# A graph attention layer on one core: the third weight slice as seven 128-cubed products per block product, PSUM in pairs of banks, ten weight sums kept resident

## The chip, the cores and the metric

The kernel runs on one core of a Trainium2 chip, in float32 throughout. The metric is the device time of one execution in microseconds; a lower time is better. The engines are named as in the profile: PE (matrix products; PEld is its weight load), DVE (vector), ACT (activation), POOL (GpSimd), SP (issues most of the DMAs).

## The reference

```python
# x: (128, 128, 768), adj: (128, 128, 128), Wq/Wk/Wv: (768, 768); H = 12 heads of 64
h = maximum(layernorm(x), 0)
q, k, v = (split_heads(h @ W + b) for W, b in ((Wq, bq), (Wk, bk), (Wv, bv)))
scores = einsum('bhqd,bhkd->bhqk', q, k) / 8 + beta * adj[:, None]
scores = where(adj[:, None] > 0, scores, -9e15)
out = einsum('bhqk,bhkd->bhqd', softmax(scores, -1), v)
return x + merge_heads(out)
```

## The kernel before

The 128 batch elements are worked on in 32 groups of four (`GRP = 4`, `NG = 32`). The weights' 2304 output columns are three slices of 768: `qk0` (first half of Q and K), `v`, and `qk1` (second half of Q and K). For a group and a slice, the activations form a 2 x 3 grid of blocks A00 to A12 (each 256 by 256: two batch elements by two chunks of 128 input features), the weights a 3 x 3 grid B00 to B22. A fast algorithm multiplies the grids with 15 block products instead of 18: `PRODUCTS` lists for each the activation operand (a block A.. or a sum S.. of blocks, `SUMS_A`), the weight operand (a block B.. or a sum T.., `SUMS_B`), the accumulation chain in PSUM (a, b, c or d) and the output tiles (r, j) that the chain's state is added to or subtracted from.

In the slices `qk0` and `v` each block product is split once more, into seven products of 128-cubed blocks ("zones") in place of eight (`product_z`, matmuls at line 495). That needs four further inner sums of the activation operand, which POOL makes (`inner`, lines 418 to 421), and seven prepared parts of the weight operand, which are made once (`prepare`), stored in DRAM, and streamed in again for every group through a ring of five tiles (`load_T`, line 297; `RING = 5`). The chain's state takes two PSUM banks (zones 0 to 3 and 4 to 6). An output tile is opened by copies from PSUM (lines 508 to 517) and then added to (DVE, lines 521 and 522). When its last product is in, POOL decodes the zones into Q and K or V (`decode`, lines 540 to 556); that is put off to the following product's slot by `later`.

In the slice `qk1` each block product is four matmuls of 256 columns per half of the output rows with resident weights (`product`, matmuls at line 571): its state takes one PSUM bank, tiles are opened by two ACT copies (line 581) and added to by one DVE instruction (line 587), and nothing has to be decoded. PE's array is used in two halves of 64 columns in all of these.

The order of the work is written out by hand. A slice is run as 15 slots, one block product each (`run`): the product's matmuls, then the steps that `then` put at that slot, then what is due (`weighing`, `overdue`), then the additions from PSUM, then the slot's "post" steps. Within an engine instructions are issued in this order. Scores of a half of the heads (`scores`, lines 609 to 616) follow early in the next slice; attention of a pair of heads (`attend`, line 646) is started at the slots `AV_AT` in `qk1` and `AV_Z` in `qk0`, and its matmuls are put singly between those of the products (`turn`). `weigh` (lines 623 to 630) divides by the softmax sums: three small DVE instructions and four ACT copies per half tile. For the next group the same slots hold the normalisation of x (`norm`, ACT), its transposition (`to_hT`, DVE line 406), the sums (`sum_acts`, DVE line 411) and the statistics of the group after (`row_stats`).

```python
AV_AT = (5, 8, 11)
AV_Z = (7, 9, 12)
ZORDER = (0, 4, 2, 8, 1, 6, 5, 3, 10, 7, 13, 9, 11, 12, 14)
free = deque(psum.tile([P, W], F32, name=f"bank{i}") for i in range(8))
take, give = free.popleft, free.append
```

The first group runs all three slices without the fast algorithm (`plain_slice`), while the weight sums are prepared. The last group's `qk1` slice has its attention and its last half-tile stores worked in.

Of the kernel before, what the change touches and what calls it, by code (L numbers as in the profile page):

```python
# [96 lines left out]
HOME = {"B00": "T12", "B10": "T10", "B02": "T0", "B20": "T4", "B11": "T13"}  # L97

SC_AT = 1
AV_AT = (5, 8, 11)
AV_Z = (7, 9, 12)
# [3 lines left out]
ZORDER = (0, 4, 2, 8, 1, 6, 5, 3, 10, 7, 13, 9, 11, 12, 14)  # L107
RING = 5

LAST = (0, 1, 2, 3, 5, 7, 6, 10, 11, 9, 4, 12, 8, 13, 14)  # L110
# [4 lines left out]
def direct(ctx, tc, x, adj, wq, bq, wk, bk, wv, bv, beta, out, bad):  # L115
# [34 lines left out]
    xg, xp, A, SP, biasT, vt, qk = {}, {}, {}, {}, {}, {}, {}  # L150

    def home_x(G, g):
        if not g % 2:
            xp[G, g // 2] = work.tile([P, 2 * NB, QD], F32, tag="x", name=f"x_{G}_{g}", bufs=2)
        t = xg[G, g] = xp[G, g // 2][:, (g % 2) * NB:(g % 2 + 1) * NB, :]
        return t

    def load_x(G, r):
        for g in range(2):
            home_x(G, 2 * r + g)  # L160
        src = x[G * GRP + 2 * r:G * GRP + 2 * r + 2].rearrange("g (b i) (a f) -> a i (g b) f", i=SQ, a=NB)
        for a in range(NB):
            nc.sync.dma_start(xp[G, r][a * SQ:(a + 1) * SQ], src[a])


    for g in range(2):
        t = home_x(0, g)
# [3 lines left out]
    ident = const.tile([P, P], F32, name="ident")  # L171
    make_identity(nc, ident)
    mean8 = const.tile([P, NB, SQ], F32, name="mean8")
# [6 lines left out]
    seen = const.tile([P, 20], F32, name="seen")  # L180

    over = const.tile([P, 44], F32, name="over")
# [7 lines left out]
    spbuf = const.tile([P, len(PRODUCTS), GRP, P], F32, name="spbuf")  # L190
# [8 lines left out]
    def flat(lo, hi):  # L199
        return spbuf[:, lo:hi].rearrange("p s g n -> p (s g n)")  # L200

    def raw_qk(u, t, parts):

        v = t.rearrange("p (c i j n) -> p c i j n", c=NC, i=2, j=3)
        for lo, hi in parts:
            for i, name in enumerate(("q", "k")):
                load_cols(nc.sync, v[:, :, i, lo:hi].rearrange("p c j n -> p c (j n)"), name, (lo + 3 * u) * P)
# [4 lines left out]
    def raw_v():  # L212
        t = flat(9, 15).rearrange("p (c n) -> p c n", c=NC)
        load_cols(nc.sync, t, "v", 0)
        for k in range(3):
            own = work.tile([P, GRP, P], F32, tag="xo", name=f"v_B{k}2", bufs=3)
            own = own.rearrange("p (c i) n -> p c (i n)", c=2)
            load_cols(nc.sync, own, "v", 4 * P, slice(2 * k, 2 * k + 2))
            for j in range(3):
                b = t[:, 2 * k:2 * k + 2, j * 2 * P:(j + 1) * 2 * P] if j < 2 else own  # L220
                wt["v", f"B{k}{j}"] = b.rearrange("p c (i n) -> p c i n", i=2)
# [7 lines left out]
    def sum_weights(sl, n):  # L229
        name, a, b, sign = SUMS_B[n]  # L230
        if (sl, name) not in wt:
            raw = [r for r, home in HOME.items() if home == name]
            if raw:
                wt[sl, name] = wt[sl, raw[0]]
            else:
                wt[sl, name] = const.tile([P, 2, 2, P], F32, name=f"{sl}_{name}")
        sum_to(nc.vector, wt[sl, name], wt[sl, a.strip("-")], a[0] == "-", wt[sl, b], sign)


# [5 lines left out]
    def prepare(sl):  # L245

        def home(n):
            return work.tile([P, 7, P], F32, tag="T", name=f"prep_{sl}_{n}", bufs=RING)

        def rest(n, t, b11, b12, b22):  # L250
            nc.vector.tensor_tensor(t[:, 6], b12, b11, ALU.subtract)
            nc.vector.tensor_tensor(t[:, 2], b22, b12, ALU.subtract)
            nc.gpsimd.tensor_tensor(t[:, 1], t[:, 4], t[:, 6], ALU.subtract)
            nc.gpsimd.tensor_tensor(t[:, 5], t[:, 3], t[:, 1], ALU.subtract)
            k = kept[sl, n] = dram.tile([P, 7, P], F32, name=f"kept_{sl}_{n}")
            nc.sync.dma_start(k, t)
# [3 lines left out]
        def sums(name):  # L260
            for out, a, b, sign in SUMS_B:
                if out == name:
                    if out not in made:
                        made[out] = home(int(out[1:]))
# [3 lines left out]
        def finish(name):  # L268
# [4 lines left out]
            else:  # L273
                t, b = home(n), wt[sl, name]
# [14 lines left out]
    ring = [(G, sl, n) for G in range(1, NG) for sl in ("qk0", "v") for n in ZORDER]  # L289
# [9 lines left out]
    raw_qk(0, flat(0, 9), ((0, 1),))  # L299
    load_x(0, 1)  # L300
    raw_qk(0, flat(0, 9), ((1, 3),))
# [14 lines left out]
    def stats(G, g):  # L316

        if G not in st:
            st[G] = stat.tile([P, GRP * NB, nc.vector.BN_STATS_DIM], F32, tag="st", name=f"st_{G}", bufs=2)
# [6 lines left out]
    def moments_1(G, lo, hi):  # L326
# [3 lines left out]
        pm[G, lo] = bank[:, 0:4 * n].rearrange("p (s b h) -> p s b h", s=2, h=2)  # L330
# [3 lines left out]
        mean = stat.tile([P, n], F32, tag="mean", name=f"mean_{G}_{lo}", bufs=2)  # L334
        nc.vector.tensor_reduce(mean, pm[G, lo][:, 0], AX.X, ALU.add)
        d = stat.tile([P, n, 2], F32, tag="dev", name=f"dev_{G}_{lo}", bufs=2)
# [5 lines left out]
    def moments_2(G, lo, hi, mean, d):  # L342
# [5 lines left out]
        ve = stat.tile([P, n], F32, tag="ve", name=f"ve_{G}_{lo}", bufs=2)  # L348
# [3 lines left out]
        r = stat.tile([P, n], F32, tag="rstd", name=f"rstd_{G}_{lo}", bufs=2)  # L352
        nc.gpsimd.tensor_tensor(r, ve, nhalf.to_broadcast([P, n]), ALU.pow)
        t = stat.tile([P, n], F32, tag="shift", name=f"shift_{G}_{lo}", bufs=2)
# [46 lines left out]

    def to_hT(G, r, k):
        name = f"A{r}{k}"
        t = A[G, name] = work.tile([P, 2, H2], F32, tag=name, name=f"{name}_{G}", bufs=1 + (name in ("A01", "A02")))
# [3 lines left out]
    def sum_acts(G, n):  # L408
        name, a, b, sign = SUMS_A[n]
# [815 lines left out]
```

## Time and profile before

| | |
|---|---|
| time, median of 3 runs | 2779.53 us (2778.94 to 2780.74) |
| profiled execution, its time | 2781.26 us |
| its span in the profile | 2779.2 us |
| PE busy | 2744.4 us, 46433 matmuls |
| DVE busy | 2187.9 us |
| POOL busy | 2297.7 us |
| ACT busy | 1363.2 us |
| DMA | 660.87 MB, 238 GB/s on average |

The span is what the profiler recorded between the first and the last instruction; the execution's own time is 2.1 us more. Busy shares are averages over the whole span. Timeline lines give the start in us from the span's start, the length, the engine, the line of the kernel, the operation, what it writes and reads, and in brackets the idle time ahead of it with what ended it. "x4" counts instructions; a matmul of float32 shows as two records, and each block product is done for both halves of the array, so four records are one 128-cubed product.

### The profile page before, as it was taken

To read this page: it belongs to the slowest core of one execution; us is meant where nothing else is said; L and a number is where in the kernel's file an instruction comes from. 1 tells how busy PE (TensorE), PEld (TensorE's weight loads), DVE (VectorE), ACT (ScalarE), POOL (GpSimd) and SP (SyncE) were. 2 spreads that over 40 slices of the span, in tenths; PEclk is the share of its full clock that TensorE was granted. 3 is DMA by queue.
4 is the path that set the end of the run, shared out by engine and by line. 5 is a ranking of instruction groups with operands and counts; after the bars stand their busy time and mean duration, and the time that the engine had idled before them with its cause. 6 is when DMAs were issued, how large, how long until landed. Compare 5 with 4: busy or idle time off the path is not lost.

```text
span 2779.2 us, 113442 instructions
## 1 busy us (share of the span) xinstructions
PE 2744.4 (99%) x46433; PEld 2401.3 (86%) x46433; DVE 2187.9 (79%) x4826; ACT 1363.2 (49%) x3999; POOL 2297.7 (83%) x4054
## 2 busy tenths in 40 slices
PE   8989999999999999999999999999999999999998
PEld 7678888899889998888989888988889989889887
DVE  5788878788878787787888787888787877878865
ACT  2445454555454554444554545554545544445543
POOL 3688988888988889888889888889888898888893
PEclk9999999999999999999999999999999999999999
DMA  8878878887878788778888788878787887788854
GB/s 212 232 239 235 237 236 236 267 251 230 239 228 258 253 249 237 234 232 264 255 238 233 233 239 268 255 228 242 226 261 253 249 234 237 231 265 253 232 185 129
DMA packets 526216, 660.87 MB, mean 238 GB/s; under 512 B 105460, under 2 KB 401664, under 8 KB 525696
## 3 DMA queue, kind: packets, MB, share of 16 engines
q1 hardware_dynamic: 525368, 653.20, 78.5%
q8 instruction: 368, 6.03, 0.9%
q14 instruction: 152, 1.25, 0.1%
q10 hardware_dynamic: 328, 0.40, 0.1%
HBM read 589.26 MB, written 64.21 MB: 235 GB/s over the span
## 4 chain that ended last, share of the span: by engine, by line


## 5 line engine op out<-in xcount | busy, mean ns | idle before, releaser
L630 ACT ACTIVATE o<-bank,sm 128x64 f32<-128x64 f32 x1524 | 354.7, 316 | 656.7 <-DVE sm L624 464.8
L495 PE MATMUL bank<-spbuf,T_qk 128*64 128x128 f32 x7440 | 660.6, 273 | 1.3 <-POOL spbuf L419 1.2
L495 PE MATMUL bank<-T_v,spbuf 128*64 128x128 f32 x7440 | 647.2, 273 | 0.1
L646 PEld LDWEIGHTS bank<-v,e 128*64 128x64 f32 x6048 | 419.3, 137 | 106.0 <-issue 0.8
L495 PEld LDWEIGHTS bank<-T_v,spbuf 128*64 128x64 f32 x7440 | 459.0, 137 | 0.4 <-ACT o L630 0.4
L495 PEld LDWEIGHTS bank<-spbuf,T_qk 128*64 128x64 f32 x7440 | 441.1, 137 | 2.1 <-POOL spbuf L419 1.4
L646 PE MATMUL bank<-v,e 128*64 128x65 f32 x6048 | 438.2, 221 | 0.2 <-ACT o L630 0.2
L495 PE MATMUL bank<-S,T_qk 128*64 128x128 f32 x4092 | 402.7, 274 | 2.5 <-DMA T_qk<-kept_qk 1.0
L495 PE MATMUL bank<-T_v,S 128*64 128x128 f32 x4092 | 402.0, 274 | 1.7 <-DVE v L521 0.7
L571 PE MATMUL bank<-S,wqk 128*64 128x256 f32 x2976 | 389.7, 380 | 0.0
L581 ACT ACTIVATE qk<-bank,bqk 128x256 f32<-128x256 f32 x372 | 156.6, 475 | 470.5 <-PE bank L571 362.2
L613 DVE SCALAR_TENSOR_TENSOR e<-bank,biasT 128x512 f32<-128x512 f32 x378 | 240.3, 685 | 90.4 <-PE bank L609 90.1
L571 PE MATMUL bank<-S,qk_T 128*64 128x256 f32 x2480 | 305.9, 379 | 0.0
L656 POOL TENSOR_TENSOR xo<-xo,o 128x512 f32<-128x512 f32 x189 | 242.4, 1283 | 50.0 <-ACT o L630 50.0
L551 POOL TENSOR_TENSOR v<-v 128x128 f32<-128x128 f32 x186 | 97.9, 526 | 224.5 <-DVE v L521 224.5
L495 PEld LDWEIGHTS bank<-T_v,S 128*64 128x64 f32 x4092 | 259.8, 137 | 8.8 <-issue 6.1
L521 DVE TENSOR_TENSOR v<-v,bank 128x512 f32<-128x512 f32 x310 | 211.7, 683 | 70.2 <-PE bank L495 60.5
L521 DVE TENSOR_TENSOR qk<-qk,bank 128x512 f32<-128x512 f32 x310 | 210.5, 679 | 68.0 <-PE bank L495 32.7
L495 PEld LDWEIGHTS bank<-S,T_qk 128*64 128x64 f32 x4092 | 249.1, 137 | 12.6 <-issue 4.6
L587 DVE TENSOR_TENSOR qk<-qk,bank 128x512 f32<-128x512 f32 (+1 forms) x311 | 207.8, 669 | 41.8 <-PE bank L571 31.5
L616 ACT ACTIVATE e<-e 128x512 f32<-128x512 f32 x378 | 230.7, 630 | 19.7 <-DVE e L613 17.9
L571 PEld LDWEIGHTS bank<-S,qk_T 128*64 128x64 f32 x2480 | 167.9, 137 | 58.9 <-issue 0.2
(164 smaller groups left out, 5923.3 us busy)
## 6 DMA issues: line engine op xcount, KB each, us to landing
T_qk<-kept_qk SPq DMA_DIRECT2D x465, 448.0 KB, 5.1
T_v<-kept_v SPq DMA_DIRECT2D x465, 448.0 KB, 4.8
x<-in_x_dram SPq DMA_DIRECT2D x254, 192.0 KB, 4.7
xo<-in_x_dram SPq DMA_DIRECT2D x189, 256.0 KB, 5.2
out_dram<-xo SPq DMA_DIRECT2D x189, 256.0 KB, 5.0
half<-in_x_dram SPq DMA_DIRECT2D x232, 192.0 KB, 3.8
adj<-in_adj_dram SPq DMA_DIRECT2D x128, 64.0 KB, 2.5
kept_qk<-prep_qk SPq DMA_DIRECT2D x15, 448.0 KB, 3.0
```

The lines of the kernel that those rows point to most:

```text
L495: nc.tensor.matmul(p[z // 4][q:q + HD, z % 4, :], lhs[:, q:q + HD], rhs, start=(first and z % 4 == 0), stop=True, skip_group_check=True)
L521: nc.vector.tensor_tensor(t[:, 0:4], t[:, 0:4], p[0], op)
L551: e.tensor_tensor(v[:, 0:2, 0:HD], heads(0), heads(3), ALU.add)
L571: nc.tensor.matmul(p[q:q + HD, i, :], lhs[:, q:q + HD], rhs, start=(first and i == 0 and c == 0), stop=(c == 1), skip_group_check=True)
L581: opened[0] = nc.scalar.activation(t[:, i, :], p[:, i, :], AF.Identity, bias=bqk[:, i, oc:oc + 1], scale=float(sign))
L587: added[G] = nc.vector.tensor_tensor(t[:, :, cols], t[:, :, cols], p[:, :, cols], ALU.add if sign > 0 else ALU.subtract)
L613: taken[0] = nc.vector.scalar_tensor_tensor(e, ps[oc, i].rearrange("p (g n) -> p g n", g=GRP), SCORE_CAP * ISCALE, biasT[G], op0=ALU.min, ...
L616: nc.scalar.activation(e, e, AF.Exp, scale=1.0 / ISCALE)
L630: nc.scalar.activation(o[:, b], pa[:, b, 0:HD], AF.Copy, scale=t[:, 1, b:b + 1])
L646: nc.tensor.matmul(pa[q:q + HD, 2 * g + i, :], es[G, oc, i][:, 2 * r + g, q:q + HD], vt[G, "v", r, h // 4][:, 4 * g + h % 4, :], start=Tru ...
L656: nc.gpsimd.tensor_add(t, t, o.rearrange("p a (b j) d -> p (a b) (j d)", j=2))
```

## The change

The slice `qk1` is done with `product_z` like the others, in an order of its own (`QORDER`); its 15 weight operands are prepared too. Ten of the 45 prepared weight operands stay in SBUF (`RESIDENT`), the other 35 are streamed for each group. To make room, the sums S.. live in one buffer that first holds the raw weights, tiles of x and of scores have fewer buffers, and the banks of PSUM are handed out in four pairs. The inner sums of a sum S.. are no longer made by POOL: an activation block A.. is kept with its eight parts, POOL makes the four further parts of the six blocks A.. only, and DVE adds whole tiles of eight parts. The additions from a pair are one instruction. `weigh` handles a whole pair at once, and the running maximum over the softmax sums becomes one reduction per group. The order written out by hand is changed throughout: attention starts at other slots, and x, its statistics and its transposition move from `qk1` into `v` in part. The end of the last group is arranged anew.

```diff
-AV_AT = (5, 8, 11)
-AV_Z = (7, 9, 12)
+AV_AT = (3, 6, 10)
+AV_Z = (4, 8, 11)
...
+QORDER = (1, 4, 0, 8, 5, 2, 10, 3, 6, 7, 13, 9, 11, 12, 14)
+ORDER = {"qk0": ZORDER, "v": ZORDER, "qk1": QORDER}
+RESIDENT = (3, 8, 12, 17, 21, 26, 30, 35, 39, 44)
...
-    free = deque(psum.tile([P, W], F32, name=f"bank{i}") for i in range(8))
-    take, give = free.popleft, free.append
+    pairs = deque(psum.tile([P, 2, W], F32, name=f"pair{i}") for i in range(4))
+    take, give = pairs.popleft, pairs.append
...
-    ring = [(G, sl, n) for G in range(1, NG) for sl in ("qk0", "v") for n in ZORDER]
+    ring = [(G, sl, n) for G in range(1, NG) for sl, n in sequence if (sl, n) not in resident]
...
-    def sum_acts(G, n):
-        name, a, b, sign = SUMS_A[n]
-        t = work.tile([P, 2, H2], F32, tag=name, name=f"{name}_{G}", bufs=1)
-        nc.vector.tensor_tensor(t, A[G, a], A[G, b], ALU.add if sign > 0 else ALU.subtract)
-        A[G, name] = t
-    def inner(G, n):
-        a = A[G, PRODUCTS[n][0]]
-        t = SP[G, n] = spbuf[:, ZORDER.index(n)]
-        e = nc.gpsimd
-        e.tensor_tensor(t[:, 0], a[:, 0, N:H2], a[:, 1, N:H2], ALU.add)
-        e.tensor_tensor(t[:, 1], t[:, 0], a[:, 0, 0:N], ALU.subtract)
-        e.tensor_tensor(t[:, 2], a[:, 0, 0:N], a[:, 0, N:H2], ALU.subtract)
-        e.tensor_tensor(t[:, 3], a[:, 1, 0:N], t[:, 1], ALU.subtract)
+    def sum_acts(G, name):
+        _, a, b, sign = [row for row in SUMS_A if row[0] == name][0]
+        t = full[G, name] = sbig[:, SPOT.index(name)]
+        nc.vector.tensor_tensor(t, full[G, a], full[G, b], ALU.add if sign > 0 else ALU.subtract)
+    def inner(G, name):
+        t = full[G, name]
+        e = nc.gpsimd
+        e.tensor_tensor(t[:, 4:6], t[:, 1:2].to_broadcast([P, 2, P]), t[:, 0:4:3], ALU.subtract)
+        e.tensor_tensor(t[:, 6], t[:, 0], t[:, 5], ALU.subtract)
+        e.tensor_tensor(t[:, 7], t[:, 2], t[:, 6], ALU.subtract)
...
+        a = full[G, an]
+        streamed = (sl, n) not in resident
+        b = tz.pop((G, sl, n)) if streamed else resident[sl, n]
+        acts = [a[:, z] for z in (0, 6, 4, 2, 7, 3, 5)]
...
-                nc.vector.tensor_tensor(t[:, 0:4], t[:, 0:4], p[0], op)
-                added[G] = nc.vector.tensor_tensor(t[:, 4:7], t[:, 4:7], p[1][:, 0:3], op)
+                added[G] = nc.vector.tensor_tensor(t, t, p[:, 0:7], op)
...
-        e.tensor_tensor(v[:, 4:6, 0:HD], heads(5), heads(2), ALU.add)
-        e.tensor_tensor(v[:, 6:8, 0:HD], heads(6), heads(2), ALU.add)
+        e.tensor_tensor(v[:, 4:8, 0:HD].rearrange("p (z h) d -> p z h d", z=2),
+                        t[:, 5:7].rearrange("p z (h d) -> p z h d", d=HD),
+                        heads(2)[:, None].to_broadcast([P, 2, 2, HD]), ALU.add)
-    def product(G, sl, n, order):
...
+            bias = biasT[G].rearrange("p g n -> p (g n)")[:, None].to_broadcast([P, 2, W])
+            nc.vector.scalar_tensor_tensor(e, ps[oc], SCORE_CAP * ISCALE, bias, op0=ALU.min, op1=ALU.add)
+            give(ps[oc])
+            nc.scalar.activation(e, e, AF.Exp, scale=1.0 / ISCALE)
...
     def activations(G):
-        at_slots(to_hT, G, ((2, ("A10",)), (9, ("A12",))))
-        at_slots(sum_acts, G, ((2, (0,)), (3, (2,)), (5, (3,)), (6, (4,)), (7, (5,)), (10, (1,)), (11, (6,)), (12, (7,)),
-                               (13, (8,)), (14, (9,))))
-        at_slots(inner, G, ((6, (0,)), (7, (4,)), (8, (2,)), (9, (1,)), (10, (8,)), (11, (6,)), (12, (5,)), (13, (3,)),
-                            (14, (10,))))
+        at_slots(to_hT, G, ((1, ("A10",)), (4, ("A12",))))
+        at_slots(inner, G, ((2, ("A10",)), (5, ("A12",))))
+        at_slots(sum_acts, G, ((3, ("S8",)), (5, ("S9",)), (6, ("S2",)), (7, ("S6",)), (8, ("S10",)), (9, ("S0",)),
+                               (10, ("S3",)), (12, ("S7",))))
     def rest_of_activations(G):
-        at_slots(sum_acts, G, ((0, (10,)),))
-        at_slots(inner, G, ((0, (7,)), (1, (13,)), (2, (9,)), (3, (11,)), (4, (12,)), (5, (14,))))
+        at_slots(sum_acts, G, ((0, ("S5",)), (6, ("S14",)), (9, ("S11",))))
...
         # in the v slice, for the next group
-                then(6 + g, norm, G + 1, g)
-            for name, at in (("A01", 5), ("A00", 6), ("A02", 7), ("A11", 11)):
-                then(at, to_hT, G + 1, int(name[1]), int(name[2]))
+                then(10 + g, norm, G + 1, g)
+            at_slots(to_hT, G + 1, ((5, ("A01",)), (6, ("A00",)), (7, ("A02",)), (14, ("A11",))))
+            at_slots(inner, G + 1, ((6, ("A01",)), (7, ("A00",)), (8, ("A02",)), (14, ("A11",))))
+            then(7, load_x, G + 1, 1)
...
+                for g, at in enumerate((8, 11, 14)):
+                    then(at, row_stats, G + 2, g)
+                for g, at in enumerate((5, 8, 11, 14)):
+                    then(at, load_halves, G + 2, g)
```

More of the change, by code (lines that the diff above doesn't have):

```diff
@@ L601, in scores @@
         order = [3 * u + j for j in order]
-        ps = {(oc, i): take() for oc in order for i in range(2)}
+        ps = {oc: take() for oc in order}
         for oc in order:
@@ L753, in run @@
                 f()
-    def slice_of(G, sl, todo, order=range(len(PRODUCTS))):
-        run([product(G, sl, n, order) for n in order], todo)
     def slice_z(G, sl, todo):
-        run([product_z(G, sl, n) for n in ZORDER], todo)
+        run([product_z(G, sl, n) for n in ORDER[sl]], todo)
     def plain_slice(G, sl, todo, rows=(0, 1)):
@@ L847, in rows_2 @@
         for k in range(3):
-            n = work.tile([P, 2, P], F32, tag="e", name=f"rows_{g}_{k}", bufs=6)
+            if not k:
+                first["rows", g] = work.tile([P, 3, 2, P], F32, tag="e", name=f"rows_{g}", bufs=3)
+            n = first["rows", g][:, k]
             first["dve"] = nc.vector.tensor_scalar(n.rearrange("p c (b j) -> p c b j", b=NB), v[:, 2 * k:2 * k + 2], mv[:, 0:1], r, op0=ALU.subtract,
@@ L977, in direct @@
     for n in range(5, 18):
-        then(n, after, step, 1 + n % 2)
+        then(n, after, step, 2)
     plain_slice(0, "qk0", todo)
@@ L1097, in general @@
+    scores_half(G, 4, 1)
+    attend_half(G, 4, 0, False)
+    nc.vector.tensor_scalar(over[:, 0:NS], seen, SUM_CAP, None, op0=ALU.is_ge)
+    attend_half(G, 3, 0, True)
+    attend_half(G, 4, 1, True)
+    pf = take()
+    nc.tensor.matmul(pf[0:1, 0, 0:NS + 24], ones, over, start=True, stop=True)
+    nc.vector.tensor_reduce(bad, pf[0:1, 0, 0:NS + 24], AX.X, ALU.max)
+    ordered.close()
 @with_exitstack
```

434 lines of the change are left out of this document (186 added, 248 removed).

## The prediction

> **What bounds the kernel now.** First the page's busy times, then the engines' busy time by slice for one group in the steady middle (v, third slice, first slice of the next group), then the timelines.
>
> ```profile
> PE 2744.4 (99%) x46433; PEld 2401.3 (86%) x46433; DVE 2187.9 (79%) x4826; ACT 1363.2 (49%) x3999; POOL 2297.7 (83%) x4054
> ```
> ```profile
> 1017.90:1044.60 26.70, 26.70 (x525) 25.67 (x523) 22.07 (x48) 15.89 (x38) 18.41 (x34) 1.00 0.88 285
> 1044.60:1073.30 28.70, 28.70 (x341) 20.02 (x339) 22.20 (x54) 9.94 (x34) 26.45 (x48) 1.00 0.77 193
> 1073.30:1102.60 29.30, 29.30 (x618) 28.41 (x616) 24.11 (x50) 16.89 (x54) 27.89 (x50) 1.00 0.80 256
> ```
> Columns: length, PE, weight loads, DVE, ACT, POOL, clock, DMA share, GB/s. PE is busy for the whole of each slice at full clock, so a group of 84.7 us is PE's own work. POOL has 73 us of work in it and DVE 68: they have room on average, but POOL has 26.45 of 28.70 us in the third slice. What PE's work consists of is in its timeline:
>
> ```profile
> 1043.94 0.39 PE L495 MATMUL bank<-T_v,spbuf 128*64 128x128 f32 x4
> 1044.16 0.39 PE L495 MATMUL bank<-T_v,S 128*64 128x128 f32 x4
> 1044.38 0.39 PE L495 MATMUL bank<-T_v,spbuf 128*64 128x128 f32 x4
> 1044.59 1.90 PE L571 MATMUL bank<-S,qk_T 128*64 128x256 f32 x16
> 1046.32 1.90 PE L571 MATMUL bank<-A,wqk 128*64 128x256 f32 x16
> 1048.05 1.90 PE L571 MATMUL bank<-S,qk_T 128*64 128x256 f32 x16
> ...
> 1055.39 0.28 PE L646 MATMUL bank<-v,e 128*64 128x65 f32 x4
> ```
> Starts are 0.219 us apart for a 128-cube and 1.73 us for a whole third-slice product. The third slice starts at 1044.59 and its first attention step at 1055.39, 10.8 us in. That step needs v tiles which POOL decodes:
>
> ```profile
> 1034.29 0.46 POOL L551 TENSOR_TENSOR v<-v 128x128 f32<-128x128 f32 x1 [7.03 <-DVE v L521]
> 1034.71 0.45 POOL L552 TENSOR_TENSOR v<-v 128x128 f32<-128x128 f32 x1
> 1035.24 0.74 POOL L553 TENSOR_TENSOR v<-v 128x256 f32<-128x256 f32 x1
> ...
> 1053.12 0.45 POOL L418 TENSOR_TENSOR spbuf<-S 128x128 f32<-128x128 f32 x1
> ```
> POOL idles 7 us, then runs six v decodes without a gap from 1034.29 to 1053.12. The last is tile (1,1), because product 14, the last of the order, completes it. It ends 8.5 us into the third slice, just ahead of the attention on head pair 2, which reads (0,1) and (1,1). DVE:
>
> ```profile
> 1030.70 0.71 DVE L406 STREAM_TRANSPOSE A<-x 128x512 f32<-128x512 f32 x1 [0.52 <-ACT x L400]
> 1032.79 0.70 DVE L406 STREAM_TRANSPOSE A<-x 128x512 f32<-128x512 f32 x1
> 1048.26 0.71 DVE L406 STREAM_TRANSPOSE A<-x 128x512 f32<-128x512 f32 x1 [2.90 <-PE bank L571]
> 1049.01 0.91 DVE L411 TENSOR_TENSOR S<-A,A 128x512 f32<-128x512 f32 x1
> ```
> At 1048.26 DVE waited 2.9 us for PE with other work queued behind: it keeps program order. So a DVE instruction that waits for POOL holds back every PSUM addition behind it.
>
> **The change, part by part** (per group, of which 30 are whole ones with all three slices and a next group).
>
> PE: a third-slice product goes from 1.73 to 7 x 0.219 = 1.53 us. 15 x 0.20 = 3.0 us saved, 93 us in 31 groups. Weighed against a rule: the steps of 0.219 are measured in the slices on both sides at the same tile shapes, so this term stands. (The Trainium skill, "TensorE: Matmul & The Clock Gate", section "Back-to-back issue gap", has about 81 ns per matmul at 128 columns against 131 at 512, so shorter matmuls would save less than their length. By an estimate between its figures seven short ones would cost 1.45 times four of 256, and the run would be 360 us longer; the traced steps, 0.219 and 0.432 us for four records, do not bear it out, and I give it no chance.)
>
> POOL: the 15 inner sums of four instructions (about 1.9 us each) become 6 of three instructions. One of 256 elements (0.74 to 0.81 as L553 and its distance to the next) and two of 128 (0.42 to 0.53 apart): 1.7 us. Six more decodes of 2.85 us (L540 to L543) come. 15 x 1.9 - 6 x 1.7 = 18.3 off, 17.1 on: no change in sum. But their place changes. The inner sums of A01, A00, A02 now stand at slots 6, 7, 8 of the v slice and that of A11 at slot 14, ahead of v decodes in POOL's order; before, none were there. From v's start at 1018.1: A01 is transposed at +13.3 and A02 at +15.4 (rows above), so POOL is through the three at 13.3 + 3 x 1.7 = +18.4, against +16.2 at which the first decode began. The merged last decode step saves nothing (two of 128 are 0.83 apart, one of 256 is 0.81). So the last decode ends 2.2 + 1.7 (A11) = 3.9 us later, 12.4 us into the third slice, or 11.6 if v grows by 0.8 (below). Attention is moved forward from slot 5 to slot 3, so PE reaches the step that reads (1,1) at 4 x 1.53 + 1.3 = 7.4 plus a wait at slot 3 of 0.6 to 1.4: there product 8 writes the pair of banks that product 4 filled one slot earlier, and ACT first has to open two tiles from it, about 1.2 us each (three copies, like L514 to L517). PE then waits some 3.2 us for POOL.
>
> DVE: the sums go from 512 to 1024 elements. L411 takes 0.64 to 1.01 (mean 0.82); 128 more elements cost 0.13 us (L521 0.681 against L522 0.549). So 1024 take 1.13 to 1.49 from start to start; I take 1.28. PSUM additions: 896 elements in one go, 1.0 from start to start, instead of 0.68 + 0.55 (0.67 in the third slice). Score minima 6 x 1.14 for 12 x 0.62; the maximum L626 goes (12 x 0.37). In sum DVE stays within 1 us. But the sum S8 at slot 3 of the third slice now reads all eight parts of A10, which POOL makes after the last v decode: 11.6 + 1.7 = 13.3 us in. DVE gets there at about 6 us and stands still. Behind it are queued 8 sums (10.2), 9 additions (9.0), a transpose and the row moments (1.1), three weighings (1.2): 21.5 us. PE's slot 14 needs slot 12's addition, that is all but the last 2.0: 13.3 + 19.5 = 32.8, plus 1.5 + 0.2 for the slot. The slice becomes about 34.5 us instead of 28.7: +5.8, the saving included. In that time also falls attention's second wait: with pairs of banks there are four PSUM buffers, and its second tile takes the first one's, given back only when DVE (behind S8) and eight ACT copies (0.23 apart) are done.
>
> First slice: attention ends at slot 6; DVE's S14 sum and weighing, eight copies (1.9) and an opening (1.2) then stand before slot 8, which comes 3.2 us later: a wait of 1.0 to 1.8. Scores wait about 0.5 for POOL's decode. +1.9. V slice: additions of 1.0 beside row statistics (1.13): +0.8; bounds 0 and 1.2.
>
> DMA: 35 loads of 448 KB for 30, so 22.6 instead of 20.3 MB per group. At 93 us that is 243 GB/s, at 81.7 us 277; the v slice already moves 285 without PE waiting. Nothing; bounds 0 and 1 us per group, since SP now issues weight loads behind its waits for half tiles (2.9 us at the longest before).
>
> Head: 15 more weight sums of about 1.4 us of DVE in the plain slices (79 us of DVE work in 128 now): +12, bounds 0 and 25. Last group: -3.0, +4 for the first attention now behind slot 1, +1.9; at the end a decode (2.85) and a whole addition come on the path: +3.5. Together +6.4.
>
> Sum: 30 x (5.8 + 1.9 + 0.8) = 255, + 12 + 6 = +273. The profiled execution took 2781.3 (span 2779.2), so 3054; the median of the runs is 1.7 lower: 3052. Ends: with inner sums at 1.57, sums at 1.13 and no waits in the other slices a group costs +2.2, the run about 2860; with contended prices throughout +12.8, about 3190.
>
> **Rivals.** (1) Faster: PE stays the bound. If POOL brings (1,1) and A10 by 7.4 us into the slice, nothing queues on DVE, and 93 us go while head and tail take 16: 2702. For it: POOL and DVE sums are no larger than before. Against: six gapless decodes alone end at 8.5 us now. The turning point is a wait of 3.0 us per group. 0.12. (2) Only the first wait costs, DVE makes its queue good in the slice's waits: 3.2 + 0.6 - 3.0 = 0.8 a group, 2781 + 24 + 18, about 2820. Against: 21.5 us of DVE work left in a slice of 25.7. 0.13. (3) Weight loads come late as well: +3 us a group, about 3140 to 3200. The longer the group, the less they do. 0.05. My forecast has 0.70.
>
> **How the numbers follow.** 2702 and half of (2) lie below 2810, and 0.04 above 3170: the range 2810 to 3170 leaves out 2 in 10. About 0.2% is what a measurement here can tell: faster 0.12, same 0.02 (between rivals 1 and 2), slower 0.86.
>
> **What would show it.** Third slice near 34 us with PE idle before the first attention step (for POOL's v decode) and the second; DVE idle for 5 us or more before its first sum there; first slice 1 to 2 us longer. 128-cubes 0.219 apart in the third slice. It is wrong if the third slice is 25.7 us with a full PE, or if PE's waits name the weight loads.

## The result and the profile after

The changed kernel takes 3329.08 us (median of 4 runs, 3326.08 to 3334.09), the kernel before 2779.9 us beside it: a ratio of 1.198, interval 1.196 to 1.200. The direction was forecast, the size was not: +549 us instead of +273. The profiled execution took 3334.09 us, with a span of 3332.2.

The page's busy times, and then the windows of one group's three slices (first slice, v, third slice; columns as in the prediction: length, PE, weight loads, DVE, ACT, POOL, clock, DMA share, GB/s):

```profile
PE 2850.5 (86%) x52005; PEld 2689.8 (81%) x52005; DVE 2222.3 (67%) x3089; ACT 1357.6 (41%) x3632; POOL 2352.0 (71%) x3339
```
```profile
1579.40:1615.90 36.50, 31.49 (x616) 29.65 (x614) 22.49 (x29) 15.79 (x46) 24.20 (x32) 0.95 0.61 184
1615.90:1648.40 32.50, 28.65 (x522) 27.14 (x520) 21.23 (x29) 14.48 (x27) 22.66 (x40) 0.95 0.87 250
1648.40:1681.80 33.40, 28.22 (x521) 27.25 (x518) 24.81 (x35) 12.21 (x42) 26.99 (x35) 0.95 0.83 235
```

PE, 99% busy before, is at 86%, and all three slices have grown, not only the third. The clock is 0.95 in each, where it was 1.00. PE's waits by what ended them (total us, times, longest):

```profile
PE pair L500 <- DVE v L524: 147.3, 58, 4.9
PE pair L575 <- POOL qk L542: 90.4, 30, 3.1
PE pair L623 <- ACT o L607: 87.8, 31, 6.0
PE pair L500 <- ACT qk L520: 80.8, 63, 2.3
PE pair L500 <- DVE qk L524: 25.8, 56, 0.7
```

The waits name four different late producers: DVE's additions in the v slice, POOL's decode before the scores of the first slice, ScalarE's copies that give back attention's PSUM pair, and ScalarE's openings of output tiles. In the timeline of PE, the same group:

```profile
1588.43 0.45 PE L575 MATMUL pair<-qk 64*64 64x128 f32 x8 [3.06 <-POOL qk L542]
...
1603.24 1.75 PE L500 MATMUL pair<-sbig,res_qk 128*64 128x128 f32 x28 [1.60 <-ACT qk L520]
...
1636.99 2.40 PE L500 MATMUL pair<-T_v,sbig 128*64 128x128 f32 x28 [2.05 <-DVE v L524]
1645.26 1.75 PE L500 MATMUL pair<-T_v,A 128*64 128x128 f32 x28 [1.80 <-DVE v L524]
...
1648.37 1.70 PE L500 MATMUL pair<-A,res_qk 128*64 128x128 f32 x28
1649.90 3.23 PE L500 MATMUL pair<-sbig,T_qk 128*64 128x128 f32 x56
1654.08 1.75 PE L500 MATMUL pair<-A,T_qk 128*64 128x128 f32 x28 [0.95 <-ACT qk L520]
...
1664.93 0.34 PE L623 MATMUL pair<-v,e 128*64 128x65 f32 x4 [3.37 <-ACT o L607]
1665.10 0.52 PE L500 MATMUL pair<-sbig,T_qk 128*64 128x128 f32 x4
1665.40 0.44 PE L623 MATMUL pair<-v,e 128*64 128x65 f32 x4
1665.62 0.65 PE L500 MATMUL pair<-sbig,T_qk 128*64 128x128 f32 x4
1666.04 0.44 PE L623 MATMUL pair<-v,e 128*64 128x65 f32 x4
```

The third slice's products themselves start 1.53 us apart where PE does not wait (1648.37 to 1649.90). The last lines show one thing more: the step of a zone and an attention matmul together, 0.33 us before, is 0.52 and then 0.64 us behind the wait of 3.37 us. PE runs at half clock there. The clock records of the trace hold 85 such stretches, 345 us in all, each one or more times 3.41 us; the kernel before had 6 (23 us), none in the steady groups.

**Where the time went, for one steady group** (means of 26 groups, v start to v start): 84.42 us before, 102.41 after.

| per group | us |
|---|---|
| PE's work, 15 products of 1.53 for 1.73 us | -3.0 |
| PE idle by the profile: 0.05 before, 14.46 after | +14.4 |
| end of the pipe: 8.8 waits of 0.17 (a zone lasts 0.39 us, the next could start after 0.22) | +1.5 |
| half clock: 10.24 us at half speed (at most; PE waits during 0.7 us of it) | +5.1 |
| sum | +18.0 |

The first v slice starts at 184.4 us instead of 161.1 (+23), and behind the last v slice come 51.5 us instead of 44.2 (+7).

### The profile page after: what moved, and what is told of

The parts are those of the page before. It is cut to its first block, busy times and chain, and to the rows that moved or that the text cites. A ratio compares the mean times of both kernels' runs of the same rounds, so it can differ in the third digit from the quotient of the medians.

```text
span 3332.2 us, 120955 instructions
## 1 busy us (share of the span) xinstructions
PE 2850.5 (86%) x52005; PEld 2689.8 (81%) x52005; DVE 2222.3 (67%) x3089; ACT 1357.6 (41%) x3632; POOL 2352.0 (71%) x3339
## 4 chain that ended last, share of the span: by engine, by line
PE 35%; POOL 26%; DVE 13%; DMA 13%; ACT 6%; issue 4%; SPq 1%; ACTq 0%; DVEq 0%; POOLq 0%
PE pair L500 27%; DMA half<-in_x_dram 11%; PE pair L575 5%; POOL qk L541 4%; POOL xo L634 4%; POOL qk L540 4%; POOL qk L543 3%; PE pair L623 3%; ACT o L607 3%; DVE qk L524 3%; POOL qk L542 2%; DVE sbig L419 2%; DVE strow L377 2%; POOL v L553 1%; POOL v L555 1%
## 5 line engine op out<-in xcount | busy, mean ns | idle before, releaser
L500 PE MATMUL pair<-sbig,T_qk 128*64 128x128 f32 x15624 | 1068.2, 277 | 3.2 <-ACT qk L520 1.9
L500 PEld LDWEIGHTS pair<-sbig,T_qk 128*64 128x64 f32 x15624 | 860.4, 140 | 9.5 <-issue 5.7
L524 DVE TENSOR_TENSOR qk<-qk,pair 128x896 f32<-128x896 f32 x620 | 664.5, 1080 | 303.5 <-PE pair L500 299.8
L607 ACT ACTIVATE o<-pair,sm 128x64 f32<-128x64 f32 x1524 | 332.7, 329 | 724.1 <-DVE sm L595 703.9
L623 PE MATMUL pair<-v,e 128*64 128x65 f32 x6048 | 452.9, 230 | 91.2 <-ACT o L607 87.8
L634 POOL TENSOR_TENSOR xo<-xo,o 128x512 f32<-128x512 f32 x189 | 298.1, 1577 | 327.9 <-ACT o L607 327.9
L623 PEld LDWEIGHTS pair<-v,e 128*64 128x64 f32 x6048 | 402.8, 144 | 106.8 <-ACT o L607 95.8
L500 PE MATMUL pair<-T_v,sbig 128*64 128x128 f32 x6944 | 436.8, 283 | 57.6 <-DVE v L524 56.9
L500 PEld LDWEIGHTS pair<-T_v,sbig 128*64 128x64 f32 x6944 | 405.3, 143 | 70.3 <-DVE v L524 63.9
L524 DVE TENSOR_TENSOR v<-v,pair 128x896 f32<-128x896 f32 x310 | 330.2, 1073 | 132.5 <-PE pair L500 129.4
L540 POOL TENSOR_TENSOR qk<-qk 128x256 f32<-128x256 f32 x372 | 330.1, 888 | 49.2 <-DVE qk L524 46.8
L541 POOL TENSOR_TENSOR qk<-qk 128x256 f32<-128x256 f32 x372 | 302.2, 812 | 29.2
L543 POOL TENSOR_TENSOR qk<-qk 128x256 f32<-128x256 f32 x372 | 273.0, 734 | 29.2
```

The costliest lines, as they stand in the source:

```text
L500: nc.tensor.matmul(p[q:q + HD, z, :], lhs[:, q:q + HD], rhs, start=(first and z % 4 == 0), stop=True, skip_group_check=True)
L524: added[G] = nc.vector.tensor_tensor(t, t, p[:, 0:7], op)
L540: e.tensor_tensor(t[:, 1:4:2], t[:, 1:4:2], twice(0), ALU.add)
L541: e.tensor_tensor(t[:, 2:5:2], t[:, 2:5:2], twice(1), ALU.add)
L543: e.tensor_tensor(t[:, 5:7], t[:, 5:7], twice(2), ALU.add)
L607: nc.scalar.activation(o[:, r, b], pa[:, r, b, 0:HD], AF.Copy, scale=t[:, 1, r, b:b + 1])
```

## The experiments

Steady groups are told as above; a run's ratio is to the kernel before on the same chip. e1 to e6 each act on one suspect of the changed kernel.

**e1, no half tiles loaded.**

```diff
-            nc.vector.bn_stats(rows[G][:, g, h, :], rows[G, g, h])
+            nc.vector.bn_stats(rows[G][:, g, h, :], rows[G, g, h] if G == 2 else bv_b[:, h * VH:(h + 1) * VH])
...
-                for g, at in enumerate((5, 8, 11, 14)):
-                    then(at, load_halves, G + 2, g)
```

> The changed kernel, but the half tiles of x from which the row statistics are taken are not loaded from the third group on; the same statistics instructions read a tile that is always there, and the variance is replaced by 1 (so the normalisation of these groups is left out of the result). Theory (the v slice is longer because row statistics wait for their half tiles, and the PSUM additions queued behind them on VectorE hold PE back): PE's waits at slots 10 and 13 of the v slice (2.0 to 3.3 and 1.7 us) and the half-clock stretches behind them go; the v slice falls from 33.4 to 27 to 29 us, and 5 to 6 us per group make 3329 into 3150 to 3200. Rival (the v slice is longer because PSUM additions and POOL's inner sums are too much work for it): v stays above 31 us and the run above 3270.

3239.15 us, ratio 1.165 (1.161 to 1.168). The v slice falls from 33.9 to 27.6 us, as the theory had it, but the third slice grows from 32.3 to 35.6, so only 90 us come of it and the run stays above the theory's range. In the changed kernel DVE's timeline shows the cause, the statistics standing at their loads with additions behind them:

```profile
1642.93 1.08 DVE L377 BATCH_NORM_STATS2 strow<-half 128x6 f32<-128x384 f32 x2 [2.41 <-DMA half<-in_x_dram]
...
1644.17 2.23 DVE L524 TENSOR_TENSOR v<-v,pair 128x896 f32<-128x896 f32 x2
```

PE's wait of 1.80 us ends at 1645.26, inside that pair of additions. And here is what e1 gets in the third slice, which starts at 1600.64:

```profile
1611.28 0.34 PE L624 MATMUL pair<-v,e 128*64 128x65 f32 x4 [0.95 <-POOL v L556]
...
1619.32 0.48 PE L624 MATMUL pair<-v,e 128*64 128x65 f32 x4 [3.59 <-ACT o L608]
```
```profile
1613.02 1.23 DVE L420 TENSOR_TENSOR sbig<-A,A 128x1024 f32<-128x1024 f32 x1 [6.02 <-POOL A L427]
```

That is the prediction's third slice in kind: POOL's last v decode late for attention (by 0.95 us, where some 3.2 were said), and DVE standing 6 us at the sum S8 until 12.4 us into the slice.

**e2, PE's waits filled.**

```diff
+        then((2, "post"), fill, 14, "d")
+        then((7, "post"), fill, 7, "c")
...
+            then((9, "post"), fill, 10, "c")
+            then((12, "post"), fill, 8)
...
+        then((2, "post"), fill, 4, "a")
...
+            if sl == "qk1" and n == 3 and z == 0 and G < NG - 1:
+                fill(15, chain)
```

> The changed kernel with 58 more products of 128 cubed per group, into a PSUM zone that nobody reads, placed on PE just before its five long waits (14, 7, 10, 8, 4 and 15 of them, 0.219 us each, so that each fills its wait but hardly outlasts it). Theory (PE's clock is halved for 3.4 us or more after PE has waited for 2 to 3 us, which costs some 5 us per group beside the waits themselves): with PE busy through the waits the half-clock stretches go, the mean clock rises from 0.95 to 0.99 or more, and the run falls to 3170 to 3250 though PE has 12.7 us more work per group. Rival (the clock is lowered for another reason, such as the load): the clock stays at 0.95 or falls, and the run takes 3329 to 3450.

3279.65 us, ratio 1.179 (1.176 to 1.183), mean clock 0.988. Time at half clock falls from 10.24 to 1.31 us per group, so the stretches do come of PE's waits. The run lies between the two ranges: 1.9 us per group come back instead of 3 to 5, for half clock costs 4.5 us less, but idle time and fill together are 16.9 us (4.15 and 12.7) instead of 14.5. A PE that is not slowed would arrive earlier at the next late producer and wait longer for it; that some fills simply outlast their waits is not ruled out.

**e3, one decode on VectorE.**

```diff
-                later(lambda r=r, j=j: decode(G, sl, r, j))
+                e = nc.vector if sl == "qk1" and (r, j) == (0, 0) and G < NG - 1 else nc.gpsimd
+                later(lambda r=r, j=j, e=e: decode(G, sl, r, j, e))
```

> The changed kernel with one of the six decodes of the third slice, tile (0,0), on VectorE instead of POOL. Theory (the wait of 3.4 us before the second scores of the first slice comes from POOL, which has work without a gap from the middle of the third slice): the wait goes, with the half clock behind it; the first slice falls from 36.4 to 31 to 33 us and the run to 3170 to 3240. Rival (POOL and VectorE are both late, and the wait only moves to the next score or to VectorE's additions): less than 1 us per group, 3300 to 3340.

3209.66 us, ratio 1.154 (1.151 to 1.158): -119 us. The wait for POOL is gone, the first slice takes 32.2 us instead of 36.3, and 1.0 us of wait for ScalarE stays at its slot 3. The theory holds.

**e4, attention later.**

```diff
-AV_AT = (3, 6, 10)
+AV_AT = (3, 8, 11)
```

> The changed kernel with the second and third attention of the third slice opened behind slots 8 and 11 instead of 6 and 10. Theory (PE waits 3.4 us at slot 7 because attention's second tile takes the PSUM pair that the first one gives back late, VectorE standing at the sum S8 for POOL): that wait falls to 0 to 1 us with the half clock behind it, the third slice goes from 32.5 to 28 to 30 us, the run to 3180 to 3260. Rival (VectorE's queue behind S8 is the limit; PE then waits at slots 12 to 14 for the additions): third slice above 31.5 us, run above 3300.

3243.7 us, ratio 1.167 (1.163 to 1.170). The total is the theory's, but the third slice is not: it stays at 32.9 us, its wait at slot 7 (2.7 us on average, 3.37 in the group shown) being replaced by 2.2 us on average for ScalarE's openings around slot 8 and 2.2 at attention's third step. The rival had such a slice, with waits for DVE's additions instead. What fell is the first slice, to 32.4 us: there the waits before the scores went from 3.4 to 1.0 us on average. That it is for POOL's additions of attention (L634), which come later and leave the decodes ahead of them, is argued, not tested.

**e5, half tiles four slots ahead.**

```diff
-                for g, at in enumerate((8, 11, 14)):
+                for g, at in enumerate((6, 10, 14)):
                     then(at, row_stats, G + 2, g)
-                for g, at in enumerate((5, 8, 11, 14)):
+                for g, at in enumerate((2, 6, 10, 14)):
```

> The changed kernel with the half tiles of x loaded at slots 2, 6, 10 and 14 of the v slice instead of 5, 8, 11 and 14, and the statistics taken at slots 6, 10, 14 and, as before, slot 2 of the third slice: four slots (some 7 us) between load and use instead of three. Nothing is left out. Theory (VectorE stands at the statistics because loads take 5 to 7 us and three slots are 5.3 us): the v slice falls from 33.4 us to 27 to 29 us as it did without the loads, the third slice gains some 3 us as it did there, and the run comes to 3230 to 3260. Rival (loads queued behind others on SP are late wherever they stand): v stays above 31.5 us, run above 3290.

3253.3 us, ratio 1.170 (1.166 to 1.174): v 28.9 us, third slice 34.4 us. In this slice three slots between load and use are too few and four are enough; the queue on SP was not the fault.

**e6, inner sums of A10 on VectorE.**

```diff
-        e = nc.gpsimd
+        e = nc.vector if name == "A10" and G > 1 else nc.gpsimd
```

> The changed kernel with the three inner sums of activation block A10 on VectorE instead of POOL (some 1.2 us more on VectorE, 1.7 less on POOL). Theory (VectorE stands at the sum S8 for POOL's inner sums of A10, which come behind the v decodes, and attention's second PSUM pair comes back late for that): the wait of 3.4 us at slot 7 of the third slice falls below 1 us, with the half clock behind it, and as POOL is through earlier the wait of 3.4 us for its decode in the first slice shrinks as well: 4 to 7 us per group, 3120 to 3210. Rival (VectorE has too much queued there in any case, so that its own extra work gives the time back): less than 1.5 us per group, above 3280.

3246.92 us, ratio 1.168 (1.163 to 1.173). The third slice goes from 32.3 to 29.3 us, the wait at slot 7 to 0.8 us on average (1.6 at most): S8's wait for POOL was what held attention's pair back. The first slice's wait does not shrink (3.07 us still), so that part of the theory falls, and the run is outside its range.

**e7, e3 to e6 together.**

> The changed kernel with four edits at once: decode of tile (0,0) of the third slice on VectorE, the inner sums of A10 on VectorE, attention opened behind slots 3, 8 and 11, half tiles loaded four slots ahead. Theory (the loss is a sum of waits for late producers, each of which can be taken out by itself): of 14.5 us of waits per group the openings by ScalarE (1.6 and 0.95) and some 1.5 us of others stay, 4 us, with little half clock; 82.8 + 1.2 + 4 + 0.5 = 86 to 89 us per group, 2840 to 2930. Rival (POOL and VectorE have too much work for a group of less than some 95 us in this order, and a wait taken out comes back elsewhere): 3050 to 3150.

3104.24 us, ratio 1.116 (1.111 to 1.122): 225 us less than the changed kernel, where the four by themselves give 119, 85, 76 and 82, 362 in sum. The rival's range holds it. Of 14.5 us of idle time per group 10.0 stay. Waits that were taken out do come back elsewhere, though nearly half of what stays is for ScalarE's openings (4.8 us per group instead of 2.5), an engine that the rival does not name:

```profile
PE pair L500 <- ACT qk L520: 144.4, 97, 2.2
PE pair L624 <- ACT o L608: 76.3, 31, 6.6
PE pair L624 <- POOL v L556: 39.1, 31, 2.4
```

**e8, one wait of a chosen length in the kernel before.**

```diff
+    def stall(k):
+        bank = take()
+        nc.tensor.matmul(bank[:, 0:P], idle, idle, start=True, stop=True)
+        nc.scalar.copy(idle, bank[:, 0:P])
+        for _ in range(k):
+            nc.scalar.activation(idle, idle, AF.Copy)
+        nc.tensor.matmul(bank[:, 0:P], idle, idle, start=True, stop=True)
+        give(bank)
...
+            then((9, "post"), stall, (0, 2, 4, 6, 8, 10, 13, 16)[G % 8])
```

> The kernel before, with one wait of PE made in each v slice, behind slot 9: a small product of 128 cubed, its copy by ScalarE and a chain of 0 to 16 further copies of 128x128 on ScalarE, then a small product that reads the result (it is used nowhere). The wait's length goes through eight steps from about 0.7 to about 5 us, by group. Theory (a wait of PE above some length is followed by half clock): groups with waits of 0.7 to 1.5 us show none and grow by the wait alone; from 2 to 3 us on a stretch of 3.4 us at half clock follows and the group grows by some 1.7 us more. Mean wait 2.6 us, so 2781 + 78 + 20 to 30, 2870 to 2900. Rival (the half clock of the changed kernel has another cause): no stretches at half clock, 2850 to 2865.

2931.18 us, ratio 1.054 (1.050 to 1.059), above both ranges: the waits were longer than planned (2.87 us on average, 86 us in 30 groups), the two small products and the ends of the pipe around them, some 28 us (85.74 less 84.42 and 0.35 is 0.97 per group), were not counted, and the half clock came to some 38, by the table. By length (the group's time less that of the shortest wait, less the difference of the waits, is the cost of the half clock; the first group is left out):

| PE's wait, us | groups | with half clock behind it | group, us | cost of it, us |
|---|---|---|---|---|
| 0.35 | 3 | 0 | 85.74 | 0 |
| 1.04 | 3 | 0 | 86.40 | 0.0 |
| 1.72 | 4 | 0 | 87.23 | 0.1 |
| 2.40 | 4 | 4 | 89.69 | 1.9 |
| 3.08 | 4 | 2 | 89.76 | 1.3 |
| 3.76 | 4 | 4 | 91.48 | 2.3 |
| 4.79 | 4 | 4 | 92.37 | 2.2 |
| 5.81 | 3 | 3 | 93.53 | 2.3 |

The theory holds: no wait up to 1.72 us is followed by half clock, from 2.40 us most are, for 3.4 or 6.8 us, at some 2 us each where PE is the bound. That only two of four are at 3.08 us has its reason in the last section.

**e9, ScalarE's openings kept clear** (with e3, e5 and e6).

```diff
-QORDER = (1, 4, 0, 8, 5, 2, 10, 3, 6, 7, 13, 9, 11, 12, 14)
+QORDER = (1, 4, 0, 5, 8, 2, 10, 3, 6, 7, 13, 9, 11, 12, 14)
-AV_AT = (3, 6, 10)
+AV_AT = (4, 7, 11)
-AV_Z = (4, 8, 11)
+AV_Z = (5, 8, 11)
...
-        for n, j in ((0, 2), (2, 0), (3, 1)):
+        for n, j in ((1, 2), (2, 0), (3, 1)):
             then((n, "post"), scores, G - 1, 1, (j,))
```

> The changed kernel with the decode of tile (0,0) and the inner sums of A10 on VectorE and half tiles loaded four slots ahead, and moreover with ScalarE's openings kept clear of its other work: in the third slice product 8 goes behind product 5 (so the PSUM pair opened at slot 1 is not needed at slot 3), attention is opened behind slots 4, 7, 11 there and 5, 8, 11 in the first slice, and the first slice's scores come behind slots 1, 2, 3 instead of 0, 2, 3. Nothing is left out. Theory (what is left of the waits after the four edits is mostly ScalarE: 2.2 and 1.5 us in the first slice, 0.95 and 1.6 to 2.2 in the third, and 1.0 for the last v decode): most of these 7.5 us go, a group of 94.65 comes to 87 to 90 us, the run to 2870 to 2960. Rival (each removed wait moves POOL's and VectorE's lateness to the next place): above 3040.

3052.19 us, ratio 1.098 (1.093 to 1.103). Half clock is as good as gone (0.26 us per group), ScalarE's openings of Q and K tiles cost 1.0 us instead of 4.7, but the group falls by 1.9 us only: waits for DVE's additions and for POOL before the scores of v have come up. The rival again.

**e10, the statistics' new place alone, in the kernel before.**

```diff
-                then(13, load_halves, G + 2, 0)
...
+                    for g, at in enumerate((8, 11, 14)):
+                        then(at, row_stats, G + 2, g)
+                    for g, at in enumerate((5, 8, 11, 14)):
+                        then(at, load_halves, G + 2, g)
...
-            for g, at in enumerate((2, 5, 8, 11)):
-                then(at, row_stats, G + 2, g)
-                if g < 3:
-                    then(at, load_halves, G + 2, g + 1)
...
+                then(2, row_stats, G + 2, 3)
...
-            then(13, row_moments, G + 2)
+            then(13 if G == 1 else 4, row_moments, G + 2)
```

> The kernel before, with one part of the change alone: from the fourth group on the half tiles of x are loaded at slots 5, 8, 11 and 14 of the v slice and the row statistics taken at slots 8, 11, 14 and slot 2 of the third slice, as in the changed kernel. Nothing is left out. Theory (the place of the statistics, three slots behind their loads, makes VectorE stand in the v slice whatever the rest does): the v slice goes from 26.5 to 29 to 32 us, with half clock behind the longer waits, and the run from 2780 to 2860 to 2960. Rival (it hurts only together with the heavier additions and the later engines of the changed kernel): 2775 to 2810.

2862.06 us, ratio 1.030 (1.023 to 1.037), at the lower edge of the theory's range: the v slice grows by 2.8 us, with little half clock (0.4 us per group). DVE's waits and PE's for it, in this kernel:

```profile
DVE strow L374 <- DMA half<-in_x_dram: 118.1, 95, 3.3
```
```profile
PE bank L495 <- DVE v L521: 65.2, 43, 3.5
```

So this one move costs some 82 us (63 to 102 by the interval) without anything else of the change.

**e11 to e14, what is left.** e11 is e9 with the scores later still; e12 takes the row statistics from DVE, e13 the v decodes from POOL, e14 both.

```diff
-        for n, j in ((1, 2), (2, 0), (3, 1)):
+        for n, j in ((1, 2), (3, 0), (4, 1)):
             then((n, "post"), scores, G - 1, 1, (j,))
...
-        for n, j in ((0, 2), (2, 0), (3, 1)):
+        for n, j in ((1, 2), (3, 0), (5, 1)):
             then((n, "post"), scores, G, 0, (j,))
```

> The kernel of e9 (decode of tile (0,0) and inner sums of A10 on VectorE, half tiles four slots ahead, ScalarE's openings kept clear) with the scores still later: behind slots 1, 3, 4 of the first slice and 1, 3, 5 of the v slice. Nothing is left out. Theory (of the 8.8 us of waits left, the 1.65 us before scores in the v slice are for POOL's decode alone and go when it has a slot more): 1.5 to 2.5 us per group, 2970 to 3010. Rival (VectorE and POOL are full in this order, so that the wait comes back behind slots 8 to 14): 3030 to 3070.

```diff
     def row_stats(G, g):
+        if G > 2:
+            return
...
+            nc.vector.memset(ve, 1.0)
...
+            nc.vector.memset(mean, 0.0)
```

> The kernel of e11 without the row statistics and their half tiles from the third group on (mean 0 and variance 1 are put in their place, so the normalisation of these groups is left out of the result): some 4.5 us less of VectorE's work per group. Theory (VectorE has no room left: its work, with what the edits moved to it, is late at slots 8 and 14 of the v slice and 5, 13 and 14 of the third): waits of 3 to 4.5 us go, 90 to 140 us less than e11. Rival (what is left are waits of one engine for another's single late instruction, whatever VectorE's load): less than 1.5 us per group, under 45 us less than e11.

```diff
         nv[0] += 1
+        if 1 < G < NG - 1:
+            return
```

> The kernel of e11 without POOL's decodes of the six v tiles of a group from the second to the last but one (attention there reads the tiles of an earlier group, so its result is left out): some 17 us less of POOL's work per group. Theory (POOL and VectorE are both late and hide behind each other): as with the statistics left out, little changes, less than 1.5 us per group, 2990 to 3035. Rival 1 (POOL alone is the limit): 4 us per group or more, below 2915. Rival 2 (single late instructions of ScalarE and VectorE hold the rest): 2990 to 3035 here too, but then e14 stays above 2960.

> The kernel of e11 without the row statistics and their half tiles and without the v decodes (both as in e12 and e13; the normalisation and the attention result of these groups are left out). Theory (POOL and VectorE are both late and hide behind each other): the waits for v decodes and for VectorE's additions go together; of 7.6 us the 2.0 for ScalarE in the first slice and 1 to 2 others stay, 86 to 89 us per group, 2830 to 2920. Rival (single late instructions of ScalarE and VectorE hold the rest): above 2960.

| us | with v decodes | without |
|---|---|---|
| with row statistics | 3034.32 (e11) | 3022.53 (e13) |
| without | 3025.73 (e12) | 2934.95 (e14) |

e11 gains 18 us on e9, about 0.5 per group; the rival's range holds it. Each relief alone brings 9 and 12 us, hardly clear of the spread of e11's two runs (10 us), both together 99. e12's theory, that DVE alone has no room left, falls: it expected 90 to 140 us less. PE's idle time per group says the same less sharply: 8.2 us in e11, 7.6 in e12, 7.4 in e13, 5.15 in e14. Some of what a single relief wins is lost to half clock, which goes from 0.5 us per group in e11 to 2.9 in e12 and 1.7 in e13 (1.05 in e14). PE's longest waits in e11:

```profile
PE pair L500 <- DVE qk L524: 81.8, 86, 1.8
PE pair L500 <- ACT qk L520: 62.7, 32, 2.0
PE pair L624 <- ACT o L608: 58.7, 33, 6.6
```

In e12 the waits for DVE's additions shrink to 51 us and those for ScalarE's copies (o) to 9, and a wait for POOL's last v decode stands in their place, where the prediction had named one:

```profile
PE pair L632 <- POOL v L564: 87.1, 31, 3.4
PE pair L508 <- ACT qk L528: 62.2, 32, 2.1
PE pair L508 <- DVE qk L532: 51.1, 59, 1.4
```

With both reliefs (e14) it is gone:

```profile
PE pair L508 <- ACT qk L528: 60.1, 32, 2.1
PE pair L508 <- DVE qk L532: 34.6, 35, 2.0
PE pair L634 <- ACT o L618: 22.2, 33, 5.9
```

The theory's interaction is there; e14 is 15 us above the theory's range and 25 below the rival's, since 5.15 us of waits stay per group: for ScalarE's openings, for some of DVE's additions, and 32 us in the run for weight loads. POOL and DVE are both too late in this order, and each hides the other. No version came below the kernel before.

## Why the prediction was right or wrong

- **PE's work: right.** The third slice's products start 1.53 us apart. The rule that made short matmuls dearer (the Trainium skill, "TensorE: Matmul & The Clock Gate", section "Back-to-back issue gap") is not borne out: seven of 0.219 us are 1.53.
- **First slice, +1.9: it grew by 7.1.** The wait for ScalarE at slot 8 was sized right (1.60, said 1.0 to 1.8). The step that failed is "Scores wait about 0.5 for POOL's decode": it is 3.06 and 0.35 us. POOL goes through this part without idling, and an addition of attention in its queue takes 2.26 us:

```profile
1581.27 2.26 POOL L634 TENSOR_TENSOR xo<-xo,o 128x512 f32<-128x512 f32 x1
1583.49 0.73 POOL L540 TENSOR_TENSOR qk<-qk 128x256 f32<-128x256 f32 x1
...
1587.93 0.46 POOL L542 TENSOR_TENSOR qk<-qk 128x128 f32<-128x128 f32 x1
```

  PE's scores start at 1588.43, as that last instruction ends. e3 takes one decode out and gets 4.1 us back.
- **V slice, +0.8: it grew by 7.3.** The step that failed is "additions of 1.0 beside row statistics (1.13)": it priced the statistics' own work and not their load. They stand three slots behind their loads, as most did in the kernel before. But there both were in the third slice: DVE came for a load 5.4 us after its issue, the load had landed after 3.3 us (means of 152 and 133 loads), and DVE waited 1.2 us in the run. Loads issued in the v slice land later: in e10 after 4.7 us (mean of 78), when DVE comes after 4.3 us (mean of 150). In the changed kernel DVE stands for the DMA 205 us in the run (102 times, up to 4.5 us), with the additions behind it. Why loads land later in the v slice is not tested; the weights that are streamed there are the obvious suspect. The prediction looked for DMA trouble at the weight loads, and there PE hardly waits (0.7 us in the run). That the load is the cause, e1, e5 and e10 show from three sides.
- **POOL's inner sums ahead of the v decodes: right.** The first v decode was put 18.4 us into the v slice, which starts at 1615.93; it is 19.1:

```profile
1634.57 0.46 POOL L426 TENSOR_TENSOR A<-A 128x128 f32<-128x128 f32 x1
1634.98 0.46 POOL L551 TENSOR_TENSOR v<-v 128x128 f32<-128x128 f32 x1
```

- **Third slice, +5.8: it grew by 3.6.** The mechanism was right and its place too (slot 3 waits 0.95, said 0.6 to 1.4; S8 waits for POOL's inner sums; attention's second tile for the pair), but the longer v slice gives POOL time to finish: the first attention step, for which 3.2 us were said, does not wait at all. Where v has its normal length, in e1, DVE stands until 12.4 us into the slice (said 13.3) and the slice takes 35.6 us (said 34.5). That these come so close is partly luck: the first attention step waits 0.8 us there on average, and the slice has 4.3 us at half clock, which the sum lacks. e6 shows that S8's wait is the cause of the second wait.
- **Not in the prediction at all: half clock**, 5.1 us per group by its time, of which 1.9 come back when most of it is removed (e2).
- **Head +12 and last group +6.4**: +23, with the first slice of the first whole group included, and +7. The head was not examined further.
- **The rivals.** PE stays the bound (2702), or DVE makes its queue good (2820): both need POOL and DVE to have room in their order. e14, with 17 us of POOL's work and some 5 of DVE's left out per group, still takes 2935. Late weight loads: PE waits 0.7 us for them in the changed kernel, and a total of 3140 to 3200 would have been nearer for a wrong reason; as the group gets shorter they come up (20 us in e7, 32 in e14), the way the prediction said they would depend on its length.

In sum, the waits that the prediction saw were sized fairly, but for that of the first attention step, and two that it priced near nothing, a moved load and a decode queue, with the clock that follows them, make up the other half.

## What to carry to other kernels

When an edit moves an instruction that reads a load, price the load's time to land and the distance from its issue to its use, both in the new place, and name what is queued behind it on its engine. Where PE is 99% busy only because POOL and DVE are just in time, a small saving on PE buys waits: removing one of them shows the next, so the sum of the single gains (362 us here) is no forecast for all of them together (225). Count PE waits of 2 us and more with some 2 us of slow clock on top where PE is the bound (e8), and with less where another engine is late next (1.9 us for 8.9 us at half clock in e2).

## What the hardware showed

- Half clock follows shorter waits than expected: in e8 2.40 us every time, 1.72 us never. What decides is not the length of a wait but PE's idle time within a window. All changes of the clock in the 16 traces lie on a grid of 3.413 us. Counted from 190 us on, a window at full clock in which PE was idle for 2.1 us or more was followed by one at half clock each time (398 of 398), one with less than 1.6 us almost never (3 of 12272), one in between 92 times of 355. At half clock, the next window was a full one when PE was idle for less than 0.8 us (480 of 497) and never otherwise (0 of 66). In e8 each wait of 2.40 us happened to put 1.8 us or more into one window; the two of 3.08 us without half clock lie across a border of the grid, 1.60 and 1.48 us, 1.55 and 1.54 us. The Trainium skill ("TensorE: Matmul & The Clock Gate", section "HAM oscillation — how this bites in real kernels") warns of gaps above about 3.4 us; the stretches' length of 3.41 us or a multiple agrees with its window, the threshold does not: here some 2.1 us of idle time in a window is enough.
- POOL is stretched by DVE's sums of two SBUF tiles and not by DVE's additions from PSUM. In the changed kernel 94 decode instructions of POOL (L540, L541, L543) last 1.70 us on average instead of 0.73, and all 94 lie beside a sum of line 419, of the 1022 short ones 118, while 557 of the short ones lie beside an addition from PSUM (line 524). Of its additions L634, 58 last 2.26 us, all beside such a sum, and 131 last 1.27, four of them. The Trainium skill ("GPSIMD Engine Reference", section "Key points") says that POOL contends with DVE instructions that have two SBUF inputs; the trace agrees.
